# A graph-attention kernel: loads in order of need, and k and v of two batches made beside the first graph weights

## The chip, the cores and the metric

The kernel runs on one core of a Trainium2 chip. The core has a matrix engine (PE), a vector engine (DVE), an activation engine (ACT), a general engine (POOL) and a queue engine (SP) that issues most of the transfers; ACT and POOL can issue transfers too. The engines run side by side, each takes its own instructions in the order in which the program has them, and they wait for one another on semaphores. The metric is the device time of one execution in microseconds (us), the median of several runs.

## The reference, cut to what matters

Two layers on x of shape (16, 1024, 256), with an adjacency matrix adj of (1024, 1024), all float32. Each layer adds its result to x and normalises the rows. The change touches layer 0 only.

```python
# layer 0, for each of 16 batches
c = mean(x, axis=-1)                                  # one number per node
diff = c[None, :] - c[:, None]
A = abs(abs(sigmoid(diff) - 0.5) - 0.5) * 2
Wg = adj * (A + A.T) / 2                              # the graph weights, 1024 x 1024
q = relu((x.T @ Wg) * para)                           # 256 x 1024
k, v = split(x @ kv_w)
out = softmax(q_h.T k_h * scale) @ v_h                # 4 heads of 64
x = layernorm(x + out)
# layer 1: a graph convolution with adj, two linear layers and two batch norms
```

The graph weights of a batch depend on its x only through the row means c. Since 1 - tanh(|d|/2) = 2 (1 - sigmoid(|d|)), a weight block is made with an Abs, a Tanh and one product with adj.

## The kernel before

P = 128 partitions, N = 1024 nodes in NCH = 8 blocks, C = 256 channels in CC = 2 blocks. `fast_path` is the part that runs; a second path, for softmax sums out of range, stands behind a test and does not run here. All loads of layer 0 go to SP's queue at the start:

```python
def load_x(b):
    t = xp.tile([P, NCH, C], F32, tag="x", name=f"x_{b}")
    nc.sync.dma_start(t, x[b].rearrange("(n p) c -> p n c", p=P))
    st[b] = {"x": t}

load_x(0)
nc.sync.dma_start(adj_s, adj.rearrange("(n p) m -> p n m", p=P))
nc.sync.dma_start(kvw_s, kv_w.rearrange("(c p) k -> p c k", p=P))
nc.sync.dma_start(para_s, para.rearrange("o (c p) i j -> p (o c) (i j)", p=P))
```

Each batch has a prologue in three lists: `first` (four transposes of x; the first of them also starts the row means), `steps` (v and k, then the graph matmuls that give q) and `side` (the graph weights). The row means lie one per partition (ccol); the Abs also needs them as a row in every partition (crow). They go there through DRAM: a write of 1024 single floats, then a read that repeats the row in 128 partitions.

```python
def begin():                                          # called by transpose_x(0, 0)
    s["xT"] = xTp.tile(...)                           # xTp has one buffer
    csum = small.tile([P, NCH], F32, tag="csum", name=f"csum_{b}")
    nc.vector.tensor_reduce(csum, xt, AX.X, ALU.add)
    nc.vector.tensor_scalar(s["ccol"], csum, 1.0 / C, None, ALU.mult)
    nc.vector.tensor_scalar(ncol, csum, -1.0 / C, None, ALU.mult)
    nc.sync.dma_start(c_d[b].rearrange("o (n p) -> p (o n)", p=P), ncol)
    s["crow"] = crp.tile([P, N], F32, tag="crow", name=f"crow_{b}")      # crp has one buffer
    nc.sync.dma_start(s["crow"], c_d[b][0].partition_broadcast(P))

def transpose_x(c, half):
    if c == 0 and half == 0:
        begin()
    pt = tile_t(f"pxT_{b}_{c}_{half}")                # tile_t: two PSUM buffers
    for j in range(4):
        nc.tensor.transpose(pt[...], xt[:, 4 * half + j, c * P : (c + 1) * P], ident)
    nc.vector.tensor_copy(s["xT"][:, c, half * HALF : (half + 1) * HALF], pt)

def weights_abs(n):                                   # wgp has 8 buffers
    nc.scalar.activation(w, s["crow"], AF.Abs, bias=s["ccol"][:, n : n + 1])
def weights_tanh(n):
    nc.scalar.activation(w, w, AF.Tanh, scale=0.5)
def weights_adj(n):
    nc.vector.scalar_tensor_tensor(w, w, 1.0, adj_s[:, n, :], op0=ALU.subtract, op1=ALU.mult)

# keys(kc, half): 2 matmuls to a tile_t buffer, copied to kT by ACT
# values(pair):   4 matmuls to a tile_t buffer, copied to v by DVE
# graph_mm(c, half, part): x times the weights, 8 blocks summed in a tile_t buffer; then
#                 DVE multiplies by para into qT and ACT takes the Relu
```

Attention runs in "bursts" of two units, 16 bursts a batch (u = 0 to 15). A unit is one 128 x 1024 block of scores, its exp on ACT (read from one of two PSUM buffers) and its product with v; DVE sums the exps. Four p buffers hold the exps. Into the bursts of batch b the rest of the work is woven: the weights of b+1 (`side`), its k, v and q (`steps`), and the transposes of b+2.

```python
FULL = (0, 4, 6, 8, 10, 12)
SIDE = {13: 2, 14: 2, 15: 2, 1: 2, 2: 2, 3: 2}
load_x(1)
first, steps, side = prologue(0)
run(first, 4)
while steps:
    run(side, 6)
    run(steps, 2)
next_first, next_steps, next_side = prologue(1)
run(next_first, 4)
run(next_side, 6)
...
for j in range(len(bursts)):
    b, u = j // PERB, j % PERB
    for i in bursts[j]:
        scores(i)                                     # matmuls and exps of this burst
    ...
    if u == 0:
        steps, side = next_steps, next_side
    if j:
        back(j - 1)                                   # products with v and sums of the burst before
    if u == 5 and b + 2 < B:
        load_x(b + 2)
        next_first, next_steps, next_side = prologue(b + 2)
    if u in FULL:
        if u >= 10:
            run(next_first, 1)
        else:
            run(full.get(j, []), 9)
        for _ in range(4):
            run(steps, 1)
            if u <= 4:
                run(side, 2)
        if u >= 10:
            run(next_first, 1)
            run(full.get(j, []), 9)
    elif u > 12:
        run(next_side, SIDE[u])
    else:
        run(side, SIDE.get(u, 0))
```

So in before the row means of batch b+2 start at u = 10 and the first Abs that reads them comes at u = 13. PE, ACT and DVE keep the order in which the program calls them.

Of the kernel before, what the change touches and what calls it, by code (L numbers as in the profile page):

```python
# [10 lines left out]
F32 = mybir.dt.float32  # L11
# [7 lines left out]
P = 128  # L19
# [496 lines left out]
def fast_path(  # L516
# [96 lines left out]
    with (  # L613
# [16 lines left out]

        def load_x(b):
            t = xp.tile([P, NCH, C], F32, tag="x", name=f"x_{b}")
            nc.sync.dma_start(t, x[b].rearrange("(n p) c -> p n c", p=P))
            st[b] = {"x": t}

        load_x(0)
        nc.sync.dma_start(adj_s, adj.rearrange("(n p) m -> p n m", p=P))
        nc.sync.dma_start(kvw_s, kv_w.rearrange("(c p) k -> p c k", p=P))
        nc.sync.dma_start(para_s, para.rearrange("o (c p) i j -> p (o c) (i j)", p=P))
        load_columns()  # L640

        def prologue(b):


            s = st[b]
            xt = s["x"]
            first, steps, side = [], [], []

            def step(f, *a):
                steps.append((f, a))  # L650

            def begin():
                s["xT"] = xTp.tile([P, CC, N], F32, tag="xT", name=f"xT_{b}")


                csum = small.tile([P, NCH], F32, tag="csum", name=f"csum_{b}")
                nc.vector.tensor_reduce(csum, xt, AX.X, ALU.add)
                s["ccol"] = small.tile([P, NCH], F32, tag="ccol", name=f"ccol_{b}")
                nc.vector.tensor_scalar(s["ccol"], csum, 1.0 / C, None, ALU.mult)
                ncol = small.tile([P, NCH], F32, tag="ncol", name=f"ncol_{b}")  # L660
                nc.vector.tensor_scalar(ncol, csum, -1.0 / C, None, ALU.mult)
                nc.sync.dma_start(c_d[b].rearrange("o (n p) -> p (o n)", p=P), ncol)
                s["crow"] = crp.tile([P, N], F32, tag="crow", name=f"crow_{b}")
                nc.sync.dma_start(s["crow"], c_d[b][0].partition_broadcast(P))

            def transpose_x(c, half):
                if c == 0 and half == 0:
                    begin()
                pt = tile_t(f"pxT_{b}_{c}_{half}")
                for j in range(4):  # L670
                    nc.tensor.transpose(
                        pt[:, j * P : (j + 1) * P], xt[:, 4 * half + j, c * P : (c + 1) * P], ident
                    )
                nc.vector.tensor_copy(s["xT"][:, c, half * HALF : (half + 1) * HALF], pt)


            def weights_abs(n):
                w = wgp.tile([P, N], F32, tag="wg", name=f"wg_{b}_{n}")
                nc.scalar.activation(w, s["crow"], AF.Abs, bias=s["ccol"][:, n : n + 1])  # L679
                s["wg", n] = w  # L680

            def weights_tanh(n):
                w = s["wg", n]
                nc.scalar.activation(w, w, AF.Tanh, scale=0.5)  # L684

            def weights_adj(n):
                w = s["wg", n]
                nc.vector.scalar_tensor_tensor(  # L688
                    w, w, 1.0, adj_s[:, n, :], op0=ALU.subtract, op1=ALU.mult
                )  # L690

            def graph_mm(c, half, part):
                if part == 0:
                    s["pg"] = tile_t(f"pg_{b}_{c}_{half}")
                    if c == 0 and half == 0:
                        s["qT"] = qkv.tile([P, CC, N], F32, tag="qT", name=f"qT_{b}")
                ps = s["pg"]
                hs = slice(half * HALF, (half + 1) * HALF)
                for n in (2 * part, 2 * part + 1):
                    nc.tensor.matmul(  # L700
                        ps, xt[:, n, c * P : (c + 1) * P], s["wg", n][:, hs],
                        start=(n == 0), stop=(n == NCH - 1),
                    )
                if part == 3:
                    q = s["qT"][:, c, hs]
                    nc.vector.scalar_tensor_tensor(  # L706
                        q, ps, -scale, para_s[:, c, hs], op0=ALU.mult, op1=ALU.mult
                    )
                    nc.scalar.activation(q, q, AF.Relu)  # L709

            def keys(kc, half):
                if kc == 0 and half == 0:
                    s["kT"] = qkv.tile([P, CC, N], F32, tag="kT", name=f"kT_{b}")
                ps = tile_t(f"pk_{b}_{kc}_{half}")
                hs = slice(half * HALF, (half + 1) * HALF)
                for c in range(CC):
                    nc.tensor.matmul(
                        ps, kvw_s[:, c, kc * P : (kc + 1) * P], s["xT"][:, c, hs],
                        start=(c == 0), stop=(c == CC - 1),
                    )  # L720
                nc.scalar.copy(s["kT"][:, kc, hs], ps)  # L721

            def values(pair):
                if pair == 0:
                    s["v"] = qkv.tile([P, NCH, C], F32, tag="v", name=f"v_{b}")
                pt = tile_t(f"pv_{b}_{pair}")
                for j in range(2):
                    n = 2 * pair + j
                    for c in range(CC):
                        nc.tensor.matmul(  # L730
                            pt[:, j * C : (j + 1) * C], s["xT"][:, c, n * P : (n + 1) * P],
                            kvw_s[:, c, C : 2 * C], start=(c == 0), stop=(c == CC - 1),
                        )
                nc.vector.tensor_copy(  # L734
                    s["v"][:, 2 * pair : 2 * pair + 2, :].rearrange("p n c -> p (n c)"), pt
                )

            for c in range(CC):
                for half in range(2):
                    first.append((transpose_x, (c, half)))  # L740
            for i in range(4):
                step(values, i)
                step(keys, i // 2, i % 2)
            for c in range(CC):
                for half in range(2):
                    for part in range(4):
                        step(graph_mm, c, half, part)
            for n in range(NCH):
                side.append((weights_abs, (n,)))
                side.append((weights_tanh, (n,)))  # L750
                if n:
                    side.append((weights_adj, (n - 1,)))
            side.append((weights_adj, (NCH - 1,)))
            return first, steps, side
# [115 lines left out]
        FULL = (0, 4, 6, 8, 10, 12)  # L870
        SIDE = {13: 2, 14: 2, 15: 2, 1: 2, 2: 2, 3: 2}
        with tc.manual_schedule(engines={mybir.EngineType.PE, mybir.EngineType.Activation, mybir.EngineType.DVE}):
            load_x(1)
            first, steps, side = prologue(0)
            run(first, 4)
            while steps:
                run(side, 6)
                run(steps, 2)
            next_first, next_steps, next_side = prologue(1)
            run(next_first, 4)  # L880
            run(next_side, 6)
            full, quarter, late = {}, {}, {}

# [14 lines left out]
# [3 lines that stand above are left out]
                    scores(i)  # L901
                run(quarter.get(j, []), 9)
                if u == 0:
                    steps, side = next_steps, next_side
                    next_first, next_steps, next_side = [], [], []
                if j:
                    back(j - 1)
                run(late.get(j, []), 9)
# [5 lines that stand above are left out]
                        run(next_first, 1)  # L914
                    else:
                        run(full.get(j, []), 9)
                    for _ in range(4):
                        run(steps, 1)
                        if u <= 4:
                            run(side, 2)  # L920
                    if u >= 10:
                        run(next_first, 1)
                        run(full.get(j, []), 9)
# [4 lines that stand above are left out]
# [284 lines left out]
```

## Time and profile before

| | |
|---|---|
| time, median of 3 runs | 2909.42 us (2908.18 to 2910.81) |
| span of the profiled run | 2908.0 us |
| PE busy | 2702.1 us (93%) |
| DVE busy | 1444.5 us (50%) |
| ACT busy | 1138.5 us (39%) |
| POOL busy | 185.8 us (6%) |
| moved by DMA | 169.00 MB, mean 58 GB/s |

The page of the profile gives for each engine its busy time, and the span in 40 equal slices (72.7 us each), a digit per slice: the busy share in tenths. Groups of instructions follow: line, engine, operation, output and inputs, count, then busy time, mean of one in ns, and the idle time of the engine before them with what ended it. A timeline lists instructions by start: start in us, duration, engine, line, operation, and in brackets how long the engine had been idle and what released it. "SPq" rows are issues of transfers, and their durations are those of issuing, not of the transfer. In a list of stretches each engine's busy time is followed by its number of instructions in brackets. PE durations are modelled, and consecutive ones may overlap.

### The profile page before, as it was taken

How to read it: one execution, taken by the hardware profiler on the slowest of the kernel's cores; microseconds unless marked ns; L12 is line 12 of the kernel's file. 1: busy time of each engine (PE TensorE's matmuls, PEld its weight loads, DVE VectorE, ACT ScalarE, POOL GpSimd, SP SyncE). 2: the span in 40 equal slices, each digit the busy share in tenths (PEclk: the TensorE clock that was granted, in tenths of full speed). 3: DMA queues.
4: the chain of work that ended last, by engine and by line, in shares of the span. 5: the costliest groups of instructions: out<-in, count | busy, mean ns of one | idle time of the engine just before them, and what ended most of it. 6: DMA issues, size and time to landing. Idle time of an engine off the chain costs nothing. (4 is left out here: it accounts for less than half of the span.)

```text
span 2908.0 us, 32691 instructions
## 1 busy us (share of the span) xinstructions
PE 2702.1 (93%) x13522; PEld 1200.7 (41%) x13522; DVE 1444.5 (50%) x2130; ACT 1138.5 (39%) x1313; POOL 185.8 (6%) x196
## 2 busy tenths in 40 slices
PE   5899999999999999999999998799999999999842
PEld 2344443444444444444443446444444444344332
DVE  2456666656656756765765655411112112333464
ACT  2444644554553653653563542010111001233473
POOL 0000000000000000100000001000000000000032
PEclk8899999999999999999999997799999999999955
DMA  4001011011011101101101011022121111334165
GB/s 130 8 8 30 9 37 30 9 36 38 16 23 37 30 9 37 30 8 37 30 9 38 16 51 39 15 87 116 72 87 68 76 73 58 130 145 161 70 222 199
DMA packets 122062, 169.00 MB, mean 58 GB/s; under 512 B 86704, under 2 KB 103600, under 8 KB 111664
## 3 DMA queue, kind: packets, MB, share of 16 engines
q1 hardware_dynamic: 112720, 99.70, 11.3%
q0 software_dynamic: 9184, 67.12, 5.9%
q8 instruction: 108, 1.77, 0.3%
q14 instruction: 50, 0.41, 0.0%
HBM read 99.36 MB, written 67.44 MB: 57 GB/s over the span
## 5 line engine op out<-in xcount | busy, mean ns | idle before, releaser
L779 ACT ACTIVATE p<-ps 128x1024 f32<-128x1024 f32 x512 | 495.0, 1019 | 151.9 <-PE ps L774 82.8
L774 PE MATMUL ps<-qT,kT 64*64 64x512 f32 x4096 | 496.4, 599 | 12.1 <-ACT p L779 12.1
L795 PE MATMUL po<-p,v 64*64 64x512 f32 x4096 | 486.9, 589 | 0.0
L804 DVE TENSOR_TENSOR acc<-acc,p 128x1024 f32<-128x1024 f32 x384 | 469.9, 1224 | 26.0 <-ACT p L779 3.5
L700 PE MATMUL pg<-wg,x 128*128 128x512 f32 x1024 | 451.4, 594 | 1.6 <-ACT kT L721 1.6
L1024 PE MATMUL pagg<-ahT,x1l 128*128 128x512 f32 x1024 | 444.1, 593 | 0.0
L1043 ACT ACTIVATE hw<-ph,col_b 128x1024 f32<-128x1024 f32 x64 | 71.3, 1114 | 657.1 <-PE ph L1039 657.1
L1024 PEld LDWEIGHTS pagg<-ahT,x1l 128*128 128x128 f32 x1024 | 194.4, 191 | 241.1 <-issue 241.1
L700 PEld LDWEIGHTS pg<-wg,x 128*128 128x128 f32 x1024 | 189.7, 190 | 231.9 <-issue 216.5
L795 PEld LDWEIGHTS po<-p,v 64*64 64x64 f32 x4096 | 162.6, 133 | 277.8 <-issue 277.1
L774 PEld LDWEIGHTS ps<-qT,kT 64*64 64x64 f32 x4096 | 148.9, 133 | 299.9 <-issue 225.8
L709 ACT ACTIVATE qT<-qT 128x512 f32<-128x512 f32 x64 | 40.4, 631 | 529.8 <-DVE qT L706 529.8
L1103 PE MATMUL po<-hl,w2T 128*128 128x512 f32 x512 | 222.8, 598 | 6.9 <-ACT hl L1094 6.9
L1028 DVE COPY agg<-pagg 128x1024 f32<-128x1024 f32 x32 | 39.2, 1225 | 377.8 <-PE pagg L1024 377.8
L1039 PE MATMUL ph<-agg,w1T 128*128 128x512 f32 x512 | 222.2, 592 | 0.0
L688 DVE SCALAR_TENSOR_TENSOR wg<-wg,adj_s 128x1024 f32<-128x1024 f32 x128 | 170.9, 1353 | 50.1 <-ACT wg L684 50.1
L706 DVE SCALAR_TENSOR_TENSOR qT<-pg,para_s 128x512 f32<-128x512 f32 x64 | 44.2, 690 | 259.5 <-PE pg L700 259.5
L850 POOL TENSOR_TENSOR x<-x,o 128x512 f32<-128x512 f32 x64 | 81.0, 1266 | 1418.3 <-DVE o L845 1418.3
L730 PE MATMUL pv<-kvw_s,xT 128*128 128x256 f32 x512 | 127.0, 393 | 35.3 <-DVE v L734 25.5
L1045 DVE BATCH_NORM_STATS2 bn_st<-hw 128x6 f32<-128x512 f32 x128 | 82.4, 685 | 152.3 <-ACT hw L1043 152.3
L679 ACT ACTIVATE wg<-crow,ccol 128x1024 f32<-128x1024 f32 x128 | 147.4, 1151 | 16.7 <-DMA crow<-c 16.6
L1103 PEld LDWEIGHTS po<-hl,w2T 128*128 128x128 f32 x512 | 98.3, 192 | 131.4 <-issue 121.9
(87 smaller groups left out, 2034.9 us busy)
## 6 DMA issues: line engine op xcount, KB each, us to landing
h<-hw POOLq DMA_DIRECT2D x16, 2048.0 KB, 6.6
hl<-h SPq DMA_DIRECT2D x16, 2048.0 KB
x<-in_x_dram SPq DMA_DIRECT2D x16, 1024.0 KB
x<-x POOLq DMA_DIRECT2D x16, 1024.0 KB, 4.2
x1l<-x SPq DMA_DIRECT2D x16, 1024.0 KB
xf<-x SPq DMA_DIRECT2D x16, 1024.0 KB
out_dram<-xf POOLq DMA_DIRECT2D x16, 1024.0 KB, 5.6
crow<-c SPq DMA_DIRECT2D x16, 512.0 KB
```

The source lines that it names most:

```text
L679: nc.scalar.activation(w, s["crow"], AF.Abs, bias=s["ccol"][:, n : n + 1])
L688: nc.vector.scalar_tensor_tensor(w, w, 1.0, adj_s[:, n, :], op0=ALU.subtract, op1=ALU.mult)
L700: nc.tensor.matmul(ps, xt[:, n, c * P : (c + 1) * P], s["wg", n][:, hs], start=(n == 0), stop=(n == NCH - 1),)
L730: nc.tensor.matmul(pt[:, j * C : (j + 1) * C], s["xT"][:, c, n * P : (n + 1) * P], kvw_s[:, c, C : 2 * C], start=(c == 0), stop=(c == CC - 1),
L774: nc.tensor.matmul(ps[kh * D : (kh + 1) * D, hd * HALF : (hd + 1) * HALF], kT[r, pr, ks], qT[r, pr, qh * HALF : (qh + 1) * HALF], start=Tr ...
L779: nc.scalar.activation(p, ps, AF.Exp)
L795: nc.tensor.matmul(g["po"][kh][hd * D : (hd + 1) * D, :], s["v"][r, m, h * D : (h + 1) * D], p[r, hd * HALF : (hd + 1) * HALF], start=(m = ...
L804: nc.vector.tensor_add(g["acc"], g["acc"], p)
L1024: nc.tensor.matmul(ps[:, hs], xt[:, m, c * P : (c + 1) * P], ahT[:, m, hs], start=(m == 0), stop=(m == NCH - 1),)
L1039: nc.tensor.matmul(ps[:, hs], w1T[:, c, k * P : (k + 1) * P], t[:, c, hs], start=(c == 0), stop=(c == CC - 1),)
L1045: nc.vector.bn_stats(bn1_st[:, k, 2 * b + half, :], ht[:, k, half * HALF : (half + 1) * HALF])
L1103: nc.tensor.matmul(ps[:, hs], w2T[:, k, c * P : (c + 1) * P], ht[:, k, hs], start=(k == 0), stop=(k == HC - 1),)
```

## The change: loads in order of need, and a new order of the opening

The loads are put in the order in which the opening needs them: x of batch 0 in two halves, then kv_w, then a quarter of adj, x of batch 1, and the other quarters of adj. The row sums are taken in two halves, one for each half of x, so that the first can start when half of x is there; the transposes go half by half. For batch 0 the row means go to DRAM and back on ACT's queue, so that they don't stand behind the loads on SP's. In the opening, transposes, v and k of batch 1 are put ahead of the graph matmuls of batch 0, into the time in which ACT makes batch 0's weights, and the bursts of batch 0 hold no v and k any more, but the rest of batch 1's weights earlier.

The diff, whole but for its surrounding lines:

```diff
--- before.py
+++ after.py
@@ -630,12 +630,21 @@
 
         def load_x(b):
             t = xp.tile([P, NCH, C], F32, tag="x", name=f"x_{b}")
-            nc.sync.dma_start(t, x[b].rearrange("(n p) c -> p n c", p=P))
+            src = x[b].rearrange("(n p) c -> p n c", p=P)
+            if b == 0:
+                for n in range(0, NCH, 4):
+                    nc.sync.dma_start(t[:, n : n + 4, :], src[:, n : n + 4, :])
+            else:
+                nc.sync.dma_start(t, src)
             st[b] = {"x": t}
 
         load_x(0)
-        nc.sync.dma_start(adj_s, adj.rearrange("(n p) m -> p n m", p=P))
         nc.sync.dma_start(kvw_s, kv_w.rearrange("(c p) k -> p c k", p=P))
+        adj_src = adj.rearrange("(n p) m -> p n m", p=P)
+        for n in range(0, NCH, 2):
+            nc.sync.dma_start(adj_s[:, n : n + 2, :], adj_src[:, n : n + 2, :])
+            if n == 0:
+                load_x(1)
         nc.sync.dma_start(para_s, para.rearrange("o (c p) i j -> p (o c) (i j)", p=P))
         load_columns()
 
@@ -653,19 +662,28 @@
                 s["xT"] = xTp.tile([P, CC, N], F32, tag="xT", name=f"xT_{b}")
 
 
-                csum = small.tile([P, NCH], F32, tag="csum", name=f"csum_{b}")
-                nc.vector.tensor_reduce(csum, xt, AX.X, ALU.add)
+                s["csum"] = small.tile([P, NCH], F32, tag="csum", name=f"csum_{b}")
+
+            def row_means(half):
+                csum = s["csum"]
+                hn = slice(4 * half, 4 * half + 4)
+                nc.vector.tensor_reduce(csum[:, hn], xt[:, hn, :], AX.X, ALU.add)
+                if half == 0:
+                    return
                 s["ccol"] = small.tile([P, NCH], F32, tag="ccol", name=f"ccol_{b}")
                 nc.vector.tensor_scalar(s["ccol"], csum, 1.0 / C, None, ALU.mult)
                 ncol = small.tile([P, NCH], F32, tag="ncol", name=f"ncol_{b}")
                 nc.vector.tensor_scalar(ncol, csum, -1.0 / C, None, ALU.mult)
-                nc.sync.dma_start(c_d[b].rearrange("o (n p) -> p (o n)", p=P), ncol)
+                queue = nc.sync if b else nc.scalar
+                queue.dma_start(c_d[b].rearrange("o (n p) -> p (o n)", p=P), ncol)
                 s["crow"] = crp.tile([P, N], F32, tag="crow", name=f"crow_{b}")
-                nc.sync.dma_start(s["crow"], c_d[b][0].partition_broadcast(P))
+                queue.dma_start(s["crow"], c_d[b][0].partition_broadcast(P))
 
             def transpose_x(c, half):
                 if c == 0 and half == 0:
                     begin()
+                if c == 0:
+                    row_means(half)
                 pt = tile_t(f"pxT_{b}_{c}_{half}")
                 for j in range(4):
                     nc.tensor.transpose(
@@ -735,8 +753,8 @@
                     s["v"][:, 2 * pair : 2 * pair + 2, :].rearrange("p n c -> p (n c)"), pt
                 )
 
-            for c in range(CC):
-                for half in range(2):
+            for half in range(2):
+                for c in range(CC):
                     first.append((transpose_x, (c, half)))
             for i in range(4):
                 step(values, i)
@@ -870,14 +888,19 @@
         FULL = (0, 4, 6, 8, 10, 12)
         SIDE = {13: 2, 14: 2, 15: 2, 1: 2, 2: 2, 3: 2}
         with tc.manual_schedule(engines={mybir.EngineType.PE, mybir.EngineType.Activation, mybir.EngineType.DVE}):
-            load_x(1)
+
             first, steps, side = prologue(0)
             run(first, 4)
-            while steps:
-                run(side, 6)
-                run(steps, 2)
             next_first, next_steps, next_side = prologue(1)
+            run(steps, 4)
+            for _ in range(4):
+                run(side, 3)
+                run(steps, 1)
             run(next_first, 4)
+            for _ in range(8):
+                run(side, 2)
+                run(next_steps, 1)
+            run(steps, 99)
             run(next_side, 6)
             full, quarter, late = {}, {}, {}
 
@@ -914,10 +937,12 @@
                         run(next_first, 1)
                     else:
                         run(full.get(j, []), 9)
-                    for _ in range(4):
+                    for _ in range(4 if b or u > 4 else 0):
                         run(steps, 1)
                         if u <= 4:
                             run(side, 2)
+                    if not b and u <= 4:
+                        run(side, 8)
                     if u >= 10:
                         run(next_first, 1)
                         run(full.get(j, []), 9)
```

The new order of transposes holds for all batches: (half 0, c 0), (half 0, c 1), (half 1, c 0), (half 1, c 1). In later batches the first two stand at u = 10 and the last two at u = 12.

## The prediction

> **What bounds the kernel now.** I read the page first, then busy time by stretches of the span, then the timeline of the first 150 us and of one repeating period, then the waits.
>
> From the page, the slices and the row of the abs activation:
>
> ```profile
> PE   5899999999999999999999998799999999999842
> L679 ACT ACTIVATE wg<-crow,ccol 128x1024 f32<-128x1024 f32 x128 | 147.4, 1151 | 16.7 <-DMA crow<-c 16.6
> ```
>
> Busy time by stretches (start:end, then each engine's busy time, granted clock, DMA share):
>
> ```profile
> 0.00:92.00 92.00, 53.08 (x144) 29.06 (x144) 24.32 (x29) 22.38 (x25) 5.36 (x14) 0.89 0.38 103
> 92.00:142.00 50.00, 40.43 (x233) 17.52 (x236) 22.43 (x23) 31.05 (x34) 0.00 (x0) 0.82 0.04 11
> 142.00:1720.00 1578.00, 1562.68 (x10152) 647.31 (x10148) 1008.27 (x1323) 809.29 (x932) 110.30 (x101) 1.00 0.10 26
> ```
>
> PE is the bound: from 142 to 1720 us it idles 15.3 us in all. Only the first 142 us have room, 48.5 us of idle plus time at half clock. So a saving can come only from the opening, and from there on any wait put on PE is paid in full.
>
> The SP queue's timeline, 0 to 110 us (start, duration of issue):
>
> ```profile
> 6.96 3.79 SPq L633 DMA_DIRECT2D x<-in_x_dram  x1
> 10.80 9.43 SPq L662 DMA_DIRECT2D c<-ncol  x1
> 20.27 3.87 SPq L633 DMA_DIRECT2D x<-in_x_dram  x1
> 33.41 0.34 SPq L664 DMA_DIRECT2D crow<-c  x1
> 89.62 0.37 SPq L662 DMA_DIRECT2D c<-ncol  x1
> 100.69 0.33 SPq L664 DMA_DIRECT2D crow<-c  x1
> ```
>
> The row means (ncol) of batch 0 are ready at 9.4 us, but their write stands in SP's queue behind adj, kvw, para and x1; crow is issued at 33.4 and ACT starts at 38.2. Batch 1's round trip, with nothing else on the DMA engines, still takes 89.62 to 104.43 (ACT's start): 11.1 us for the write of 1024 single floats, 3.74 us for the broadcast back.
>
> **What the skill says.** "DMA: Bandwidth & Descriptors", section "Queues, rings and completion order": SP and ACT each own a row of rings on the same 16 engines, served in turn. So ACT's queue lets the write past the bulk, but shares the engines with it. No run yet shows this: before uses one such queue. The same page, "Specifications", calls writes under 512 B read-modify-writes; the trace agrees that they are slow: the 4-byte packets of 89.62 have all started by 92, yet crow's issue, which waits for the landing, is at 100.69. "TensorE: Matmul & The Clock Gate", "Architectural detail: the array is 16× 32×32, not 1× 128×128": ACT is strictly first in, first out. The trace agrees: the scores of burst 0 end at 95.8, their exp runs at 109.74, behind the activations that waited for crow. Same page, "Part 1: The HAM clock gate (the "warmup" mystery)": an idle PE falls to half clock; the trace has 0.66 granted in 100 to 120 us.
>
> **The change, part by part.** Work and instruction shapes are nearly kept: one csum reduction per batch becomes two halves, some loads are cut into pieces.
>
> *Opening, up to the first graph matmul.* Let T be when crow of batch 0 has landed (38.2 before). New: ncol at about 9.2 (x0 in halves, reductions of half of 2.28 us). Unloaded, c and crow take 9 to 11 plus 3.7 us, so T is 22 to 24 at best. But about 6 MB of bulk is still to move, at some 400 GB/s some 15 us, on the same engines. Sharing them in turn, I choose c landed at 21 to 29 and crow 4 to 6 us later: T = 25 to 35, middle 30 (an estimate). ACT's queue also holds the table load and the kT copies behind its wait for c; they fit while crow is in flight.
>
> From T, ACT is the bound: 8 pairs abs+tanh at 2.13 us (39.50 to 41.64) = 17.1, four kT copies ahead of the last tanh at 0.5 = 2.0, then wg_7 on DVE 1.23 and the last v copy 0.68, which frees the PSUM slot that the first graph matmul takes: T+21. Before it was 58.65, T+20.4. So batch 1's transposes, k and v fit in nearly free. The 64 records of graph matmul take 27.5 us as before (58.65 to 86.2). Their end: E = T+48.5.
>
> *From E to burst 6.* Before, scores of burst 6 begin at 142.19, 56 us after E = 86.2: transposes of x1, batch 1's round trip and k and v lie between. New: ACT alone sets the pace. The last Relu ends at E+1.5. Up to burst 5's first exp ACT runs a0..a7 and t0..t7 of batch 1 (17.1), five bursts' exps at 1.81 (9.1), one oT copy (0.5), one exp (1.0): E+29, so burst 6 begins at T+77.5. Saving: 142.2−77.5−T = 64.7−T. For T = 30: **35 us** (30 to 40 for T = 35 to 25).
>
> *Batches 2 to 15: a wait is put in.* The new transpose order makes the second half of csum belong to the third transpose. In the order of instructions on DVE and SP, batch b+2's ncol, c and crow therefore move from u=10 to u=12, while the first abs stays at u=13. The timeline of ACT in one period:
>
> ```profile
> 200.21 1.94 ACT L779 ACTIVATE p<-ps 128x1024 f32<-128x1024 f32 x2 [1.20 <-PE ps L774]
> 202.03 0.59 ACT L824 COPY drow<-den 128x512 f32<-128x512 f32 x1
> 202.50 1.17 ACT L679 ACTIVATE wg<-crow,ccol 128x1024 f32<-128x1024 f32 x1
> 203.70 1.06 ACT L684 ACTIVATE wg<-wg 128x1024 f32<-128x1024 f32 x1
> 204.66 1.92 ACT L779 ACTIVATE p<-ps 128x1024 f32<-128x1024 f32 x2
> 206.47 1.15 ACT L679 ACTIVATE wg<-crow,ccol 128x1024 f32<-128x1024 f32 x1
> 207.65 1.07 ACT L684 ACTIVATE wg<-wg 128x1024 f32<-128x1024 f32 x1
> 208.62 1.92 ACT L779 ACTIVATE p<-ps 128x1024 f32<-128x1024 f32 x2
> ```
>
> ACT has no gap here after the first line. Its schedule repeats each 107.12 us to within 0.02 us in all 14 batches. Per period, relative to before's issue of c (here 177.93): oT's addition, ahead of the new csum on DVE, starts at +12.90, csum at +13.51; half a reduction 1.15 and 0.31 for the rest: c is issued at +14.97. From issue of c to issue of crow the 14 periods took 8.50 to 10.97 us, mean 9.66. Add 3.74: crow lands at +27.2 to +29.7, mean +28.4. abs starts at +24.57 today. ACT is held 2.6 to 5.1 us, mean 3.8.
>
> PE's slack against this: burst 14's scores start at 203.33, burst 15's at 206.76, the next batch's first at 210.20. The last needs the exp begun at 208.62, whose first half ends at 209.6. Slack 0.6 us. So PE loses 3.8−0.6 = 3.2 us a batch, **45 us over 14** (28 to 63 if all latencies sat at one end). PE is full afterwards and can't get it back.
>
> *Sum:* 2909−35+45 = 2919; I add 2 us for a cold clock at the start of the graph matmuls: 2921.
>
> **Rivals.** (1) *Only the opening counts, the later round trip stays hidden.* For it: crow is issued 15 us before its use today. Against: the move to u=12 takes 15.0 us of that. It would give 2909−35 = 2874. (2) *The opening gains nothing, because ACT's queue is held up by the same bulk.* For it: SP's issue of c took 9.43 us, so issuing itself can be held up; 1024 tiny writes served in turn with 4 KB packets could take as long as before. Then T is near 38, the gain 27 (most of it is batch 1's), and the time 2929. (3) *The wait costs PE more than one slip per batch,* because ACT has little room through u=13 to u=15 and holds activations of the next weights. Then 5 us a batch, 2946. (4) *ACT makes up the delay before PE feels it*: for it speaks that ACT is only half used over the long stretch (809 of 1578 us); against it, the gapless lines above. Half the loss: 2898.
>
> **Range and chances.** The two large terms oppose each other, each with some 10 us of doubt: the opening 25 to 42, the repeated wait 30 to 60. That gives 2899 to 2945 for 8 in 10. Two per cent is 58 us: faster by that would need the whole opening gain and no repeated wait and more; slower would need over 7 us a batch with a full gain. Both 0.03.
>
> **What would show it.** In the changed profile: ACT's first abs between 25 and 35 us; k and v of batch 1 on PE before the first graph matmul, which begins near 51; burst 6 near 107. In each later period a wait of ACT's abs for crow of 2.6 to 5.1 us, some 50 us in all, and the waits of PE for ACT's exp grown from 6.8 to about 50 us; the period 110 instead of 107.12 us. Wrong if no such wait appears (then 2874), if the c write lands more slowly at u=12 than at u=10, or if crow of batch 0 lands after 35.

## The result

| | median | range | runs |
|---|---|---|---|
| before | 2909.93 us | 2908.18 to 2910.81 | 4 |
| after | 2956.64 us | 2954.38 to 2959.17 | 4 |

The changed kernel takes 1.0162 times the time of before, 95% interval 1.0144 to 1.0179: 46.7 us more. The prediction was 2921 us with a range of 2899 to 2945, so it had the sign, but the time lies outside the range.

The page of the profile after, PE's slices and the two groups that matter:

```profile
PE   6999999999999999999999998799999999999842
L792 PE MATMUL ps<-qT,kT 64*64 64x512 f32 x4096 | 511.3, 614 | 66.0 <-ACT p L797 66.0
L697 ACT ACTIVATE wg<-crow,ccol 128x1024 f32<-128x1024 f32 x128 | 147.0, 1149 | 62.0 <-DMA crow<-c 61.9
```

The first slice is fuller: 6 instead of 5. But ACT's Abs now waits 61.9 us for crow, in 14 pieces, where before it was 16.6 us in one piece, and PE waits 66.0 us for exps where it was 12.1.

Busy time by stretches of the profile after; each engine's time is followed by its count, then come granted clock, DMA share and GB/s:

```profile
0.00:92.00 92.00, 67.34 (x208) 37.09 (x208) 27.67 (x36) 25.39 (x30) 5.34 (x14) 0.93 0.37 109
92.00:142.00 50.00, 43.04 (x297) 15.22 (x294) 29.87 (x28) 35.13 (x38) 1.26 (x1) 0.93 0.02 1
142.00:1760.00 1618.00, 1555.74 (x9944) 635.10 (x9946) 993.71 (x1318) 799.88 (x918) 107.61 (x99) 0.99 0.09 25
```

In the first 92 us PE does 208 matmul records instead of 144. In the long stretch, where it idled 15.3 us, it now idles 62.3 (1618.00 − 1555.74), and its clock is no longer quite full.

SP's queue in the opening, and then ACT's queue and ACT, of the timeline after:

```profile
3.35 9.12 SPq L645 DMA_DIRECT2D adj_s<-in_adj_dram  x3
14.65 0.37 SPq L638 DMA_DIRECT2D x<-in_x_dram  x1
48.04 0.37 SPq L678 DMA_DIRECT2D c<-ncol  x1
58.91 0.34 SPq L680 DMA_DIRECT2D crow<-c  x1
```

```profile
8.74 0.40 ACTq L678 DMA_DIRECT2D c<-ncol  x1
28.74 0.34 ACTq L680 DMA_DIRECT2D crow<-c  x1
29.12 1.28 ACT L739 ACT_TABLE_LOAD   x1 [29.12 <-DMA c<-ncol]
...
34.73 0.59 ACT L739 COPY kT<-pk 128x512 f32<-128x512 f32 x1 [3.73 <-PE pk L735]
35.35 1.15 ACT L697 ACTIVATE wg<-crow,ccol 128x1024 f32<-128x1024 f32 x1
```

The write of c is issued at 8.7 us, and still lands only at 28.7. ACT's first weight starts at 35.35 us, right behind a kT copy, so crow had landed by then; before it was the table load at 38.20 and the weight at 39.50.

One repeating period after, ACT:

```profile
178.06 1.94 ACT L797 ACTIVATE p<-ps 128x1024 f32<-128x1024 f32 x2 [1.19 <-PE ps L792]
179.89 0.59 ACT L842 COPY drow<-den 128x512 f32<-128x512 f32 x1
185.05 1.15 ACT L697 ACTIVATE wg<-crow,ccol 128x1024 f32<-128x1024 f32 x1 [4.57 <-DMA crow<-c]
186.23 1.06 ACT L702 ACTIVATE wg<-wg 128x1024 f32<-128x1024 f32 x1
187.19 1.92 ACT L797 ACTIVATE p<-ps 128x1024 f32<-128x1024 f32 x2
```

and PE in the same period:

```profile
182.91 1.90 PE L813 MATMUL po<-p,v 64*64 64x512 f32 x16
188.25 3.50 PE L792 MATMUL ps<-qT,kT 64*64 64x512 f32 x16 [3.45 <-ACT p L797]
191.58 1.89 PE L813 MATMUL po<-p,v 64*64 64x512 f32 x16
```

The gapless row of ACT is broken by 4.57 us of waiting for crow; PE then waits 3.45 us for the exp. The second of the PE lines shows a thing that the prediction does not have: the 16 records of scores that follow the wait take 3.50 us where others take 1.90. The granted clock of that stretch, of one with a longer fall, and of a period without one:

```profile
188.10:191.40 3.30, 3.15 (x16) 1.04 (x20) 3.06 (x3) 3.27 (x5) 0.00 (x0) 0.50 0.00 0
413.40:420.00 6.60, 5.91 (x28) 1.78 (x32) 5.46 (x5) 6.51 (x7) 0.00 (x0) 0.50 0.00 1
640.00:646.00 6.00, 5.62 (x52) 1.66 (x56) 5.40 (x5) 5.97 (x8) 0.00 (x0) 1.00 0.01 3
```

Ten of the 14 periods have such a stretch, eight of 3.41 us and two of 6.83, together 41.0 us at half clock. The length of PE's wait, 2.71 to 4.22 us, does not decide it alone. All six waits of 3.31 us and more were followed by half clock; of the eight shorter ones four were and four were not, as these two, of which the shorter wait has the slower scores:

```profile
865.57 2.01 PE L792 MATMUL ps<-qT,kT 64*64 64x512 f32 x16 [3.27 <-ACT p L797]
1200.47 2.57 PE L792 MATMUL ps<-qT,kT 64*64 64x512 f32 x16 [2.71 <-ACT p L797]
```

So the books stand like this. Burst 6 of batch 0 began at 142.19 us before and begins at 120.06 after: the opening gained **22.1 us**. The issues of c for batches 2 to 15 then lie 112.3 us apart on average (170.81 to 1630.47 us, 13 periods) instead of 107.12: 5.2 us lost in each of 13, and some 4 in the last, **69 to 71 us** in all. 22 gained and 69 lost give the 47.

### The profile page after: what moved, and what is told of

Same layout as the page of the kernel before. It is cut to its first block, busy times and chain, and to the rows that moved or that the text cites. A ratio compares the mean times of both kernels' runs of the same rounds, so it can differ in the third digit from the quotient of the medians.

```text
span 2957.3 us, 32732 instructions
## 1 busy us (share of the span) xinstructions
PE 2722.6 (92%) x13522; PEld 1199.1 (41%) x13522; DVE 1446.1 (49%) x2146; ACT 1141.2 (39%) x1313; POOL 185.5 (6%) x196
## 5 line engine op out<-in xcount | busy, mean ns | idle before, releaser
L792 PE MATMUL ps<-qT,kT 64*64 64x512 f32 x4096 | 511.3, 614 | 66.0 <-ACT p L797 66.0
L813 PE MATMUL po<-p,v 64*64 64x512 f32 x4096 | 494.7, 597 | 0.0
L697 ACT ACTIVATE wg<-crow,ccol 128x1024 f32<-128x1024 f32 x128 | 147.0, 1149 | 62.0 <-DMA crow<-c 61.9
L1064 PEld LDWEIGHTS ph<-agg,w1T 128*128 128x128 f32 x512 | 97.3, 190 | 122.5 <-issue 122.5
```

Of the source, the lines that this page charges most:

```text
L792: nc.tensor.matmul(ps[kh * D : (kh + 1) * D, hd * HALF : (hd + 1) * HALF], kT[r, pr, ks], qT[r, pr, qh * HALF : (qh + 1) * HALF], start=Tr ...
L813: nc.tensor.matmul(g["po"][kh][hd * D : (hd + 1) * D, :], s["v"][r, m, h * D : (h + 1) * D], p[r, hd * HALF : (hd + 1) * HALF], start=(m = ...
L1064: nc.tensor.matmul(ps[:, hs], w1T[:, c, k * P : (k + 1) * P], t[:, c, hs], start=(c == 0), stop=(c == CC - 1),)
```

## The experiments

Two theories stood at the start. *W*: the whole repeated loss is the round trip that moved from u = 10 to u = 12 while its reader stayed at u = 13, with a part *C* of it that is not waiting but half clock after the gap. *O*: something else of the new order (transposes by halves, cut loads, kT copies) costs in each batch. The opening was then taken apart for itself. All ratios are to runs of before on the same chip.

| run | us | ratio to before, 95% interval |
|---|---|---|
| e1_means_early | 2887.52 | 0.9931 (0.9915 to 0.9948) |
| e2_only_late_means | 2977.74 | 1.0237 (1.0220 to 1.0254) |
| e3_abs_later | 2900.83 | 0.9976 (0.9967 to 0.9986) |
| e4_fill_gap | 2943.62 | 1.0119 (1.0102 to 1.0136) |
| e8_first_on_sp | 2889.52 | 0.9934 (0.9918 to 0.9951) |
| e5_crow_on_pool | 2888.95 | 0.9933 (0.9917 to 0.9950) |
| e6_kv_first | 2881.35 | 0.9903 (0.9887 to 0.9920) |
| e7_roundtrip_before_bulk | 2880.47 | 0.9902 (0.9885 to 0.9918) |
| e9_interleaved | 2869.51 | 0.9863 (0.9847 to 0.9880) |
| e10_loads_only | 2906.01 | 0.9990 (0.9981 to 0.9999) |

### Undo the late row means: e1_means_early

```diff
-                hn = slice(4 * half, 4 * half + 4)
-                nc.vector.tensor_reduce(csum[:, hn], xt[:, hn, :], AX.X, ALU.add)
-                if half == 0:
-                    return
+                if b < 2:
+                    hn = slice(4 * half, 4 * half + 4)
+                    nc.vector.tensor_reduce(csum[:, hn], xt[:, hn, :], AX.X, ALU.add)
+                    if half == 0:
+                        return
+                elif half == 0:
+                    nc.vector.tensor_reduce(csum, xt, AX.X, ALU.add)
+                else:
+                    return
```

> The changed kernel, but for batches 2 to 15 all row sums are taken at the first transpose (u = 10), as before the change; the opening and the order of transposes stay new. Theory W (the repeated loss is the wait of the first Abs for crow, and the clock that falls in the gap): the wait for crow in batches 2 to 15 goes to 0, the period returns to 107.1 us, only the opening's gain of 22 us is left: 2888 us. Rival O (something else of the new order costs, the transposes by halves or the cut loads): the period stays above 109 us and the time above 2915.

Measured: 2887.52 us. ACT in the period that answers to the one above:

```profile
178.37 1.94 ACT L802 ACTIVATE p<-ps 128x1024 f32<-128x1024 f32 x2 [1.19 <-PE ps L797]
180.19 0.59 ACT L847 COPY drow<-den 128x512 f32<-128x512 f32 x1
180.65 1.17 ACT L702 ACTIVATE wg<-crow,ccol 128x1024 f32<-128x1024 f32 x1
```

The Abs follows the copy with no wait, the issues of c are 107.1 us apart again (156.08, 263.18), and no half clock is recorded between 150 and 1700 us. Nine lines of source bring back 69 us (67 when each run is set against before on its own chip). Theory O is out: the order of transposes and the cut loads are all still there.

### The late row means alone: e2_only_late_means

```diff
 # in before: batches 2 to 15 only
-                    first.append((transpose_x, (c, half)))
+                    first.append((transpose_x, (i, o) if b >= 2 else (o, i)))
 ...      # and row sums by halves, c and crow issued with the second half, if b >= 2
```

> The kernel before, with one thing of the change: for batches 2 to 15 the new order of transposes with row sums by halves, so that c leaves at u = 12. Loads and opening are those of before. Theory W: the repeated loss stands alone, 14 times 4.9 us, 2979 us, period 112. Rival O: the loss needs the new opening or loads, and the time is under 2940.

Measured: 2977.74 us, 70.3 over before's 2907.44. The wait of ACT for crow is 62.2 us in 14 pieces (61.9 in after). So the loss needs nothing of the opening, and the two parts of the change add up to within 4 us: −19.9 (e1 against before) and +70.3 make +50, against 46.7 measured for both.

### More room for the round trip: e3_abs_later

```diff
-        SIDE = {13: 2, 14: 2, 15: 2, 1: 2, 2: 2, 3: 2}
+        SIDE = {14: 2, 15: 2, 1: 2, 2: 2, 3: 2}
```

> The changed kernel, but the first Abs and Tanh of the next batch stand at u = 14 instead of u = 13 (u = 13 has none, the whole list still ends at u = 4). c still leaves at u = 12. Theory W: 3.4 us more of time for the round trip, the wait falls from 4.4 to about 1 us a batch and PE, which had 0.6 us of slack, loses at most 0.5 us a batch: 2890 to 2900 us. Rival: not the place of the Abs but ACT's total of work in u = 13 to 4 sets the loss, and crowding it into one burst less leaves the time at 2950 or more.

Measured: 2900.83 us, just above the 2890 to 2900 that theory W said. ACT's and PE's waits between 150 and 1720 us, of e3:

```profile
ACT wg L697 <- DMA crow<-c: 5.6, 10, 1.1
```

```profile
PE pk L735 <- DVE o L863: 15.2, 27, 1.0
PE ps L792 <- ACT p L797: 7.6, 16, 0.5
```

The wait for crow has gone from 61.9 to 5.6 us by moving its reader one burst of 3.4 us, and PE's wait for exps is back to before's level. What is left against e1, 13 us, is mostly a new wait: PE's k matmuls wait 15.2 us for DVE's `o`, 12 us more than in e1 (3.1). The likely reason, which no run separates, is that the weights are now crowded into one burst less.

### Half clock or waiting: e4_fill_gap

```diff
+                if u == 14 and b + 2 < B:
+                    fill = tile_t(f"fill_{b}")
+                    for r in range(3):
+                        nc.tensor.matmul(fill, ident, adj_s[:, r, :HALF], start=True, stop=True)
```

> The changed kernel, with three matmuls of 128x128 by 128x512 (about 0.86 us each at full clock) put between the outputs of burst 13 and the scores of burst 15, in the place where PE waits; their result is not used. Theory C (of the 4.9 us lost per batch about 0.8 us is half clock after a gap of over 3 us): with the gap filled the clock stays at 1.0, the filling lies inside the wait, and the time falls by about 11 us to 2946 although there is more work. Rival: the 0.8 us is not the clock, and the time stays at 2957 or rises.

Measured: 2943.62 us, 13.0 less than after (10.5 less when each is set against before on its own chip), with 42 matmuls more. PE in the period, and its clock in the same stretch:

```profile
184.10 1.90 PE L813 MATMUL po<-p,v 64*64 64x512 f32 x16
185.93 2.84 PE L935 MATMUL fill<-adj_s,ident 128*128 128x512 f32 x6
189.52 2.00 PE L792 MATMUL ps<-qT,kT 64*64 64x512 f32 x16 [0.75 <-ACT p L797]
```

```profile
185.00:192.00 7.00, 6.25 (x42) 2.05 (x38) 3.44 (x4) 5.61 (x6) 0.00 (x0) 1.00 0.10 8
```

The scores after the filling take 2.00 us instead of 3.50, the clock stays at 1.00, and none of the 14 periods has a half clock, where after had it in ten of them. ACT's wait for crow is the same 61.9 us. So of the 69 us, some 13 are clock. The rest, 2943.6 − 2887.5 = 56.1, is 4.01 us a batch: the mean wait of ACT, 61.9 / 14 = 4.42, less 0.41.

The trace of after says the same batch by batch. In the periods where the clock held, the period grew by ACT's wait less 0.33 to 0.35 us, so PE's slack is about 0.34; with one half-clock stretch of 3.41 us it grew by the wait plus 0.56 to 0.85; with a stretch of 6.83 us by the wait plus 2.1. Against the periods where the clock held, the ten stretches thus cost 13.6 us, a figure that owes nothing to e4.

### ACT's own queue for the first round trip: e8_first_on_sp and e5_crow_on_pool

```diff
 # e8, on top of e1
-                queue = nc.sync if b else nc.scalar
+                queue = nc.sync
 # e5, on top of e1
-                queue.dma_start(s["crow"], c_d[b][0].partition_broadcast(P))
+                (queue if b else nc.gpsimd).dma_start(s["crow"], c_d[b][0].partition_broadcast(P))
```

> As e1_means_early, but the row means of batch 0 go to DRAM and back on SP's queue, behind all the loads, instead of on ACT's. Theory Q (ACT's own queue gains little, because the write shares the 16 engines with the bulk): crow of batch 0 is there at 35 to 40 us and the time is within 5 us of e1_means_early, perhaps better, since the kT copies on ACT no longer stand behind the wait for c. Rival (the other queue was worth its 10 us and more): the first Abs comes after 45 us and the time is 10 us or more above e1_means_early.

> As e1_means_early, but only the write of c for batch 0 is on ACT's queue; the read back of crow is on POOL's, so that ACT does not stand waiting for c and the kT copies go on. Theory: PE's 13.3 us of waiting for kT goes away and k and v of batch 0 are done by 25 us, but the first Abs still comes with crow at 33 to 36 us, and by the order of instructions batch 1's k stands behind the Abs: gain 0 to 4 us against e1_means_early. Rival (the wait of PE for ACT's copies set the start of the graph matmuls): they start 8 us or more earlier.

Measured: 2889.52 and 2888.95 us, 2.0 and 1.4 above e1. The first Abs of e8, and the read of crow and the first Abs of e5:

```profile
35.66 1.15 ACT L702 ACTIVATE wg<-crow,ccol 128x1024 f32<-128x1024 f32 x1 [16.84 <-DMA crow<-c]
```

```profile
27.47 0.58 POOL L685 DMA_DIRECT2D crow<-c  x1 [21.20 <-DMA c<-ncol]
```

```profile
34.19 1.15 ACT L702 ACTIVATE wg<-crow,ccol 128x1024 f32<-128x1024 f32 x1 [14.48 <-DMA crow<-c]
```

On SP behind all the loads, on ACT or on ACT and POOL, the first Abs came at 34 to 36 us (35.66 in e8, 33.98 in e1, 34.19 in e5). In e8 and e5 ACT did not stand behind c, so PE had k and v of batch 0 nearly done by 24 us; then it waited 18.22 and 15.85 us for a kT copy which the order of ACT puts behind three Abs and two Tanh. PE's gap (12.19 us in e1) moved and did not shrink.

### What set the start of the graph matmuls: e6_kv_first

```diff
 # on top of e5
-            run(steps, 4)
-            for _ in range(4):
-                run(side, 3)
-                run(steps, 1)
+            run(steps, 8)
             run(next_first, 4)
-            for _ in range(8):
-                run(side, 2)
-                run(next_steps, 1)
+            run(next_steps, 8)
+            run(side, 24)
             run(steps, 99)
```

> As e5_crow_on_pool, but k and v of both batches stand ahead of all the weights in every engine's order, so that PE makes them while c and crow travel, and the graph matmuls follow the weights one by one. Theory K (the start of the graph matmuls was set by PE's own 20 us of transposes, v and k after the first kT copies, not by ACT's weights): with those out of the way the graph matmuls end at the first Abs + 40 us instead of + 55, the time is 12 to 16 us under e1_means_early. Rival A (ACT's weights set it): no more than 4 us under it.

Measured: 2881.35 us, 6.2 under e1. The graph matmuls end 40.1 us after the first Abs (46.34 to 86.43), as said; but the gain of 12 to 16 was missed. Now the first Abs stands behind eight kT copies and so behind PE's k and v, and starts at 46.34 instead of 34 to 35.

### The round trip ahead of a part of the loads: e7_roundtrip_before_bulk

```diff
 # on top of e6: ACT's and POOL's queue for the first round trip replaced by SP's, and
         nc.sync.dma_start(adj_s[:, 0:2, :], adj_src[:, 0:2, :])
+        def load_rest():          # called after the first transposes of batch 0
             load_x(1)
             for n in range(2, NCH, 2):
                 nc.sync.dma_start(adj_s[:, n : n + 2, :], adj_src[:, n : n + 2, :])
             nc.sync.dma_start(para_s, ...)
             load_columns()
```

> As e6_kv_first, but c and crow of batch 0 are on SP's queue ahead of x of batch 1, three quarters of adj, para and the columns, which wait behind them. Theory L (the round trip took 26 us instead of 14 because it shares the engines with the bulk): the first Abs comes at 22 to 26 us and the time is about 10 us under e6_kv_first. Rival: the round trip is as slow alone, or x of batch 1 and adj now come too late, and the time is at or above e6_kv_first.

Measured: 2880.47 us, not told apart from e6. SP's queue of e7:

```profile
2.83 0.47 SPq L638 DMA_DIRECT2D x<-in_x_dram  x1
3.34 6.10 SPq L649 DMA_DIRECT2D adj_s<-in_adj_dram  x1
9.49 1.02 SPq L685 DMA_DIRECT2D c<-ncol  x1
10.55 4.94 SPq L649 DMA_DIRECT2D adj_s<-in_adj_dram  x1
24.53 0.34 SPq L687 DMA_DIRECT2D crow<-c  x1
```

The order of SP's queue is not the one that was wanted: x of batch 1 and a quarter of adj still go ahead of c, another quarter right behind it. Even so c landed 15 us after its issue, not 20. But by the order of e6, ACT could use crow only at 44.98. So the time says nothing of theory L, and the trace bears it out only in part; the next run lets ACT use crow when it is there.

### Both: e9_interleaved

```diff
 # on top of e7
-            run(next_steps, 8)
-            run(side, 24)
+            for _ in range(8):
+                run(side, 3)
+                run(next_steps, 1)
             run(steps, 99)
```

> As e7_roundtrip_before_bulk, but k and v of batch 1 are woven into the weights of batch 0 again (three steps of the weights, then one of k or v), so that ACT's first Abs does not stand behind all eight kT copies. Theory K2 (in e7 crow was there at about 29 us and ACT then waited for PE until 45): the first Abs comes at 28 to 30 us, the graph matmuls start about 21 us later, near 50, and end near 78 instead of 85: about 2872 us. Rival (crow is not there before 33, or PE's 14 us of k and v, begun later, set the start again): the graph matmuls end at 83 or later and the time is within 3 us of e7.

Measured: 2869.51 us, 1.4% under before and the fastest of all. ACT, then PE:

```profile
25.48 0.59 ACT L746 COPY kT<-pk 128x512 f32<-128x512 f32 x1 [2.86 <-PE pk L742]
29.91 1.15 ACT L704 ACTIVATE wg<-crow,ccol 128x1024 f32<-128x1024 f32 x1 [3.84 <-DMA crow<-c]
```

```profile
45.02 1.98 PE L742 MATMUL pk<-xT,kvw_s 128*128 128x512 f32 x4 [0.89 <-ACT kT L746]
46.84 27.63 PE L725 MATMUL pg<-wg,x 128*128 128x512 f32 x64
```

The first Abs comes at 29.91, 16.1 us for the write of c and 4.9 for crow after c's issue at 8.94. ACT works without a gap from there to 48.5, PE waits for a kT copy three times by under 0.9 us, and the graph matmuls begin 16.9 us after the first Abs. In after it was 27.2 us, from 35.35 to 62.53. Burst 6 begins at 104.37, 15.7 us before after's.

### What the loads bring alone: e10_loads_only

```diff
 # on top of e1: the engines' order of before
-            next_first, next_steps, next_side = prologue(1)
-            run(steps, 4)
-            ...
+            while steps:
+                run(side, 6)
+                run(steps, 2)
+            next_first, next_steps, next_side = prologue(1)
             run(next_first, 4)
-                    for _ in range(4 if b or u > 4 else 0):
+                    for _ in range(4):
-                    if not b and u <= 4:
-                        run(side, 8)
```

> As e1_means_early, but with the order of before for the engines: batch 1's transposes come after the graph matmuls of batch 0, its k and v in the bursts of batch 0. What is left of the change is the order of loads, the halves of x and ACT's queue for the first round trip. Theory M (the 22 us of the opening come from moving batch 1's transposes, round trip, k and v ahead; the loads bring only the 3 us by which the first Abs is earlier): 2903 to 2907 us. Rival (the loads are what pays): 2892 or less.

Measured: 2906.01 us, 2.9 under before's 2908.94. PE in the place that opens up between two pieces of batch 1's v:

```profile
88.22 1.88 PE L740 MATMUL pk<-xT,kvw_s 128*128 128x512 f32 x4
104.53 3.78 PE L753 MATMUL pv<-kvw_s,xT 128*128 128x256 f32 x8 [14.43 <-DVE v L757]
```

With all new loads, batch 1's round trip is in the open again, and PE waits 14.43 us behind it (8.78 us in before). The loads, the halves and ACT's queue alone bring 3 of the 20 us by which e1 is faster; the other 17 come only with the order of the engines' work. That order with the old loads was not run.

## Why the prediction was wrong

Two steps failed, both on the side of too fast a kernel. The first failed by its sizes and by a term left out: "So PE loses 3.8−0.6 = 3.2 us a batch, 45 us over 14". The runs show 69 to 71 us, 5 a batch, of which some 4 are waiting and 1 is half clock. The second failed by its path: "From T, ACT is the bound". PE's own chain ended 6 us after ACT's sum; with T later by 5, the opening gave 22 us instead of 35.

**The bound, right.** PE full from 142 us on, room only in front: after and the runs bear it out, and each wait put on PE in the long stretch was paid in full.

**The repeated wait, right in mechanism, mis-sized in two terms and one term missing.** It was found by reading the order of instructions, and e1, e2 and e3 show it from three sides. The sizes: ACT was held 4.42 us, not 3.8. The write of c took 9.73 us on average (8.51 to 11.23), against 9.66 assumed (the 14 periods of before give 9.62); from crow's issue to the Abs it was 4.4 us (3.40 to 5.69), against 3.74. That number came from a single round trip, whose write took 11.1 us, and it was added to the mean of all writes. In after, the six writes of over 10 us were followed by 3.4 to 3.9 us, the five of under 9 us by 5.0 to 5.7 us. The slack was about 0.34, not 0.6. This makes 14 x (4.42 − 0.34) = 57 us in place of 45. The missing term is the clock: after PE's waits of 2.7 to 4.2 us it fell to half in ten of fourteen periods, 13 us by e4. The prediction quoted the Trainium skill's "TensorE: Matmul & The Clock Gate", section "Part 1: The HAM clock gate (the "warmup" mystery)", for the opening, and allowed 2 us there, but did not apply it to the gap that it had itself predicted in each batch. That page puts the fall after an idle window of about 3.4 us. Here it agrees only roughly: all gaps of 3.31 us and more had the fall, but so had four shorter ones, down to 2.71, and the gaps of 3.05 and 3.27 had none; the measurement decides.

**The opening, too hopeful by 13 us (22 instead of 35),** in two steps.

First, T: "I choose c landed at 21 to 29 and crow 4 to 6 us later: T = 25 to 35, middle 30". The first Abs came at 35.35, at the end of the range. c's write took 20 us from its issue and crow up to 6.6: ACT's queue let the write be issued early, but it crawled beside the loads. Against SP's queue behind all of them (e8) it made c land 3 to 5 us earlier and the first Abs 0.3 to 1.7. This fits what the Trainium skill's page "DMA: Bandwidth & Descriptors", "Queues, rings and completion order", says of queues whose rings share the same engines. Rival 2 had this cause right, and its T of 38 was too late. With fewer loads around it (e9) the first Abs came at 29.91.

Second, "From T, ACT is the bound: ... T+21". It was T+27.2. ACT stood idle 3.5, 0.7 and 0.7 us between its last weights, waiting for PE. The step left out that PE's k of batch 0 could not go on before ACT's third kT copy, at T+5.3 (40.66), so that the last piece of k, batch 1's transposes with DVE's copies between them, and its k and v, 21 us of PE in a row, began only at 41.28. The sum for ACT was right; it was not the longest chain. e9, where PE had batch 0's part done before T, gives 16.9.

**From the graph matmuls to burst 6, right:** 30.0 us (90.09 to 120.06) against 29.

**Rivals.** 1 fell: ACT waits 61.9 us for crow in the later periods. 3, "the wait costs PE more than one slip per batch", said 5 us a batch and got the number by luck: it gave ACT's load as the reason, and the runs show a longer wait and the clock. 4 fell: ACT is half idle over the stretch and made up nothing beyond the slack.

**The sum again with terms read from the trace of after:** 2909.9 − 22 + 57 + 14 = 2959, measured 2956.6 (2959.2 in the profiled run). The upper end of the range, 2945, already had both terms at their worst, 25 us for the opening and 60 for the repeated wait. It failed because each term fell outside its own range: 22 and 70.

What stays open: why crow's read is slower after a quick write of c and quicker after a slow one, and why one wait of about 3 us is followed by half clock and another is not.

## What to carry to other kernels

When a producer is moved so that something can start sooner once, look where the same code puts it in every later repetition, and count the distance to its reader against the whole latency: here a round trip of 14 us through DRAM was given 10 us of distance, fourteen times. On an engine that is full, a wait of some 3 us can cost twice, as it did here in ten of fourteen periods: as waiting and as half speed after it. A few matmuls of no use in the gap buy the second part back, but moving the producer buys both. In an opening, write down each engine's own chain from the event on, and take the longest, not the one that was busiest before.

## What the runs showed that was not expected

- PE's clock fell in ten of fourteen gaps of 2.7 to 4.2 us, for 41.0 us in all, and adding three matmuls of no use to each gap made the kernel 13.0 us faster (10.5 against before on each chip).
- Writing 1024 single floats to DRAM takes 8.5 to 11.2 us from its issue to the issue of crow, which waits for it, with little beside it; amid the loads of the opening it took 18.5 to 20.0 us from ACT's queue and, issued at 10.93 us, 21 us from SP's (crow issued at 31.82), and 15 and 16 us in e7 and e9, where part of the loads stood behind it.
- Which queue carried that write moved the whole by 2 us or less (e1, e5, e8); how much was loaded ahead of and beside it, and whether ACT or PE was free to go on meanwhile, together moved it by 18 (e1 to e9).
